# Putting neighbour lists into degree order on TensorE with one-hot matrices, and clearing an array later

## The chip, the cores and the metric

The kernel runs on one core of a Trainium2 chip. The core has five engines with instruction queues of their own: TensorE (PE), VectorE (DVE), ScalarE (ACT), GpSimd (POOL) and SyncE (SP); DMA transfers are issued by SP, ACT and POOL and carried out by 16 DMA engines. The metric is the device time of one execution in microseconds (us). The time before is the median of 14 runs.

## The reference

Two graph layers over 3327 nodes with 512 features each, on the same sparse 0/1 adjacency matrix (symmetric, with a diagonal of ones, some eight neighbours a node). Cut to what matters:

```python
# layer 0: attention over neighbours, 4 heads of 128
feats  = einsum('nf,hfo->hno', x, W)
logits = lrelu(e_s[:, :, None] + e_n[:, None, :], 0.2) + NEG_INF * (1 - A)
out    = softmax(logits) @ feats + b
x      = layernorm(x + relu(out))
# layer 1: a second attention and a plain neighbour sum, each with a gate
e    = where(adj != 0, exp(-lrelu(s_left[:, None] + s_right[None, :], 0.01)), 0)
x_a  = (e / (e.sum(1) + 1e-5)) @ (x @ W_sa)
x_b  = adj @ (x @ W_gcnb) + b_gcnb
x    = layernorm(x + sigmoid(attn_a * x_a + attn_b * x_b))
```

## The kernel before

The kernel turns the adjacency matrix into lists of neighbours and then gathers rows by these lists, instead of multiplying by the matrix.

**Phase 0** reads the adjacency matrix in 7 chunks of 512 columns (the last has 256), each in 13 loads on SP's queue into 12 buffers (`at`). For each chunk PE multiplies the ones by powers of two (`make_codes`), ACT copies the sums, PE turns them (`turn_codes`), and DVE takes the largest 24 entries, decodes them and writes the neighbours' numbers into `st` (`top_codes`, `decode`, `pick`, lines 355 to 412). `st` holds for each node (partition = node within a tile of 128, second index = tile) its own number (word 0), up to 24 neighbours (words 1 to 24), its place in the group (word 25) and four attention terms of its own (words 26 to 29). Between these steps PE makes the feature rows (`features`, 26 tiles), which ACT copies out and POOL writes to `table0` in HBM; the order is the program's order on each engine (the loop at line 498), nothing is rescheduled.

**The order of degrees.** The nodes stand in two groups of 12 and 14 tiles. When the degrees of a group are known (`deg`), `rank_a` makes one-hot rows of them, and `rank_b` counts with two matrix products, a running sum on DVE and a few element-wise steps, until each node has its rank within the group (`ranki`). So tiles of nodes with like degrees come together, and each tile j needs `CAPS[j]` gathers only.

**What the lists go through.** `sort` scatters each tile's 128 rows of `st` (32 words) with one indirect DMA on POOL (`scatter`, line 137) to their ranks in a list in HBM, and one load (line 459) brings the list back as `srt`. For group 0 the scatters stand in `tasks`, of which three are issued after every feature tile (`later(3)` in `more`); the load is on POOL's queue, and behind it stand 12 gathers of the nodes' own rows of x (`own_x`). Group 0 is sorted in chunk 3 (`NC0`). For group 1 the rank comes after the last chunk; its scatters stand on POOL behind the first three tiles' gathers (`AHEAD`), and its load on SP.

**Layer 0** (loop at line 689) works through the 26 tiles in `order0`. For each tile POOL issues one indirect gather per list position (line 546) into 7 buffers of 6 rows, three tiles ahead; DVE makes the weights (`weigh_a`, `weigh_b`, lines 599 to 617), DVE and ACT multiply the gathered rows by them in place, and PE sums them up by products with the identity. Then come the norm and the columns that layer 1 needs, and the row is scattered to `table1`. **Layer 1** (loop at line 842) does the like from `table1`.

**A check on the side.** `over` has a one for each list position that a tile does not read; `covered` (line 468) multiplies it by `valid`, where a real neighbour stands there, and sets a flag that would start the dense version. `over` lies in a pool that takes the memory of `p0`, the pool of phase 0, and it is cleared and filled right after that pool's release (lines 676 to 678), ahead of the first `weigh_a` on DVE.

Of the kernel before, what the change touches and what calls it, by code (L numbers as in the profile page):

```python
# [8 lines left out]
F32 = mybir.dt.float32  # L9
# [5 lines left out]
P = 128  # L15
# [10 lines left out]
CAPS = (22, 12, 11, 10, 9, 9, 8, 8, 7, 6, 6, 5) + (22, 13, 11, 10, 10, 9, 9, 8, 8, 7, 7, 6, 5, 4)  # L26
LW = 32
ND = 25
# [48 lines left out]
def sparse_pass(  # L77
# [54 lines left out]
    own1 = dram.tile([NG[1] * P, 2, ROW], F32, name="own1")  # L132
    lists = [dram.tile([n * P, LW], I32, name=f"lists{i}") for i, n in enumerate(NG)]

# [13 lines left out]

    srt = [const.tile([P, n, LW], I32, name=f"srt{i}") for i, n in enumerate(NG)]
    ident = const.tile([P, P], F32, name="ident")  # L150
# [102 lines left out]
    )  # L253
    all1 = p0.tile([P, ND * NM], F32, name="all1")
    nc.gpsimd.memset(all1, 1.0)
    st = p0.tile([P, NT, LW], I32, name="st")
    nc.gpsimd.memset(st, 0)
    nc.gpsimd.iota(st[:, :, 0], pattern=[[P, NT]], base=0, channel_multiplier=1)
    for g, n in enumerate(NG):
        nc.gpsimd.iota(st[:, T0[g] : T0[g] + n, S + 1], pattern=[[P, n]], base=0, channel_multiplier=1)  # L260

    for s in range(2):
        for hh in range(2):
# [8 lines left out]
            nc.vector.tensor_reduce(w0[:, :, s, 2 * FO + 2 * hh : 2 * FO + 2 * hh + 2], prod, AX.X, ALU.add)  # L272
    zrow = p0.tile([1, ROW], F32, name="zrow")
    nc.gpsimd.memset(zrow, 0.0)
    nc.gpsimd.memset(zrow[:, F : F + 1], BIG)
    nc.gpsimd.dma_start(table1[N:NP, :], zrow)
    nrow = p0.tile([1, ROW], F32, name="nrow")
    nc.gpsimd.memset(nrow, 0.0)
# [28 lines left out]
    def features(t):  # L307

        i = t * P // CH
        xc = xcs[i]  # L310
        o = t * P - chunks[i]
        pf = psf.tile([P, 2, 512], F32, tag="pf", name=f"pf{t}")
        for k, hh in ((k, hh) for hh in range(2) for k in range(KT)):
            nc.tensor.matmul(  # L314
                pf[:, hh, :HC], xc[:, k, o : o + P], w0[:, k, hh, :], start=(k == 0), stop=(k == KT - 1)
            )
# [3 lines left out]
        nc.scalar.copy(st[:, t, S + 2 : S + 2 + H].bitcast(F32), pf[:, 1, F // 2 : HC])  # L320
# [105 lines left out]
    def rank_b(g):  # L426
# [10 lines left out]
        cum = p0.tile([P, ND * NM], F32, tag="cum", name=f"cum{g}")[:, :w]  # L437
        nc.vector.tensor_tensor_scan(cum, all1[:, :w], tots, 0.0, ALU.mult, ALU.add)
        nc.vector.tensor_sub(cum, cum, tots)
# [3 lines left out]
        nc.vector.tensor_reduce(rk[:, :n], cum.rearrange("p (v t) -> p t v", v=ND), AX.X, ALU.add)  # L443
        ranki = p0.tile([P, NM], I32, tag="ranki", name=f"ranki{g}", bufs=2)
        nc.vector.tensor_copy(ranki[:, :n], rk[:, :n])
        return ranki

# [6 lines left out]

    def sort(g, ranki, queue):

        put = lambda t: scatter(f"lists{g}", lists[g][:, :], ranki[:, t : t + 1], st[:, T0[g] + t, :])
        tasks.extend(lambda t=t: put(t) for t in range(NG[g]))
        tasks.append(lambda: queue.dma_start(srt[g], lists[g].rearrange("(t p) w -> p t w", p=P)))
        if g == 0:  # L460
# [7 lines left out]
    def covered():  # L468

        for g, n in enumerate(NG):  # L470
            nc.vector.tensor_scalar(valid[:, T0[g] : T0[g] + n, :], srt[g][:, :, 1 : S + 1], N, None, ALU.is_lt)
        bad = m0.tile([P, 4], F32, name="bad")
        nc.vector.tensor_reduce(bad[:, 0:1], ovf, AX.XY, ALU.max)
        nc.vector.tensor_scalar(bad[:, 0:1], bad[:, 0:1], 0.0, None, ALU.is_gt)
        nc.vector.tensor_mul(over, over, valid)
        nc.vector.tensor_reduce(bad[:, 1:2], over, AX.XY, ALU.max)
# [21 lines left out]
    for i in range(len(chunks)):  # L498
        make_codes(i)
        more(1)  # L500
        if i == NC0:
            rankis[0] = rank_b(0)
            sort(0, rankis[0], nc.gpsimd)
        turn_codes(i)
# [9 lines left out]
    rank_a(1)  # L514
    rankis[1] = rank_b(1)

    psf.release()
# [81 lines left out]
    def weigh_a(j):  # L599
        c = CAPS[j] + 1  # L600
        g, i = place(j)
        w = ws[j] = m0.tile([P, S + 1, H], F32, tag="w", name=f"w{j}", bufs=3)
        es = srt[g][:, i : i + 1, S + 2 : S + 2 + H].bitcast(F32)
        for s0, n, buf, o in got[j]:
# [61 lines left out]
    for i in range(AHEAD):  # L666
        got[order0[i]] = gather(table0, order0[i])
    sort(1, rankis[1], nc.sync)
    later(len(tasks))
    psl.release()  # L670
# [3 lines left out]
    over = x1b.tile([P, NT, S], F32, name="over")  # L674
    valid = x1b.tile([P, NT, S], F32, name="valid")
    nc.vector.memset(over, 0.0)
    for j, c in enumerate(CAPS):
        nc.vector.memset(over[:, j, c:S], 1.0)

# [9 lines left out]
    for i in range(NT + 3):  # L689
# [647 lines left out]
```

## Time and profile before

| what | us |
|---|---|
| median of 14 runs (1128.64 to 1154.78) | 1137.49 |
| the profiled execution | 1130.09 |
| its span, first to last instruction | 1128.4 |
| DVE busy | 733.0 (65%) |
| PE busy | 843.7 (75%) |
| POOL busy | 660.8 (59%) |
| ACT busy | 274.7 (24%) |
| last chunk picked, degrees of group 1 complete | 234.6 |
| ranks of group 1 ready | 241.0 |
| first weights of layer 0 | 262.3 |
| granted clock of PE, mean | 0.859 |

Times in the trace are counted from the first instruction. A row of a timeline has the start, the duration, the engine, the line of the kernel, the operation with the tiles that it writes and reads, the shapes, and in brackets the engine's idle time before it with what seems to have ended it; "issue" means that no event was found. Ends of matrix products are modelled. A busy share is a mean over stages with different limits.

### The profile page before, as it was taken

To read this page: it belongs to the slowest core of one execution; us is meant where nothing else is said; L and a number is where in the kernel's file an instruction comes from. 1 tells how busy PE (TensorE), PEld (TensorE's weight loads), DVE (VectorE), ACT (ScalarE), POOL (GpSimd) and SP (SyncE) were. 2 spreads that over 40 slices of the span, in tenths; PEclk is the share of its full clock that TensorE was granted. 3 is DMA by queue.
4 is the path that set the end of the run, shared out by engine and by line. 5 is a ranking of instruction groups with operands and counts; after the bars stand their busy time and mean duration, and the time that the engine had idled before them with its cause. 6 is when DMAs were issued, how large, how long until landed. Compare 5 with 4: busy or idle time off the path is not lost.

```text
span 1128.4 us, 10026 instructions
## 1 busy us (share of the span) xinstructions
PE 843.7 (75%) x2564; PEld 440.3 (39%) x2564; DVE 733.0 (65%) x2128; ACT 274.7 (24%) x751; POOL 660.8 (59%) x673
## 2 busy tenths in 40 slices
PE   5798862025976877987587975579896996999895
PEld 4576740012433433443244442234342442444342
DVE  4587786136565362832665685459796997989894
ACT  0121110002424231341143331122222122222322
POOL 7310437734666656677567527735766777777702
PEclk9898975557988888888698886779898998999998
DMA  9998999925766658667566616744867776666601
GB/s 323 395 382 344 360 386 370 330 39 145 195 176 185 180 161 199 185 186 235 170 190 203 195 57 182 199 112 121 193 169 188 179 188 190 178 182 187 181 29 59
DMA packets 74194, 229.31 MB, mean 203 GB/s; under 512 B 13873, under 2 KB 18145, under 8 KB 73233
## 3 DMA queue, kind: packets, MB, share of 16 engines
q0 software_dynamic: 50240, 164.52, 51.6%
q1 hardware_dynamic: 22784, 61.97, 14.6%
q10 hardware_dynamic: 1104, 2.10, 0.5%
q8 instruction: 23, 0.38, 0.1%
q14 instruction: 43, 0.34, 0.1%
HBM read 207.46 MB, written 28.54 MB: 209 GB/s over the span
## 4 chain that ended last, share of the span: by engine, by line
PE 24%; issue 15%; DVE 14%; another core or an unknown queue 8%; POOL 8%; ACT 5%; DMA 3%; DVEq 0%; POOLq 0%; ACTq 0%
PE acc L634 12%; POOL g L546 7%; DVE sw L795 6%; PE acc L812 4%; PE po L831 3%; DMA g<-table,srt 3%; ACT g L629 2%; PE pcol L650 2%; DVE g L797 2%; PE acc L623 2%; POOL out L137 1%; DVE g L631 1%; ACT xt L647 1%; PE pt L822 1%
## 5 line engine op out<-in xcount | busy, mean ns | idle before, releaser
L546 POOL DMA_INDIRECT g<-table,srt x496 | 509.5, 1027 | 245.6 <-issue 159.2
L634 PE MATMUL acc<-g,ident 128*128 128x512 f32 x536 | 251.5, 627 | 21.5 <-DVE g L631 21.5
L795 DVE SCALAR_TENSOR_TENSOR sw<-g,e,sw 128x512 f32<-128x512 f32 x242 | 181.4, 749 | 15.5 <-ACT sw L784 5.0
L634 PEld LDWEIGHTS acc<-g,ident 128*128 128x128 f32 x536 | 109.9, 205 | 167.2 <-issue 130.8
L812 PE MATMUL acc<-g,ident 128*128 128x512 f32 x294 | 137.3, 604 | 13.3 <-DVE g L797 12.1
L631 DVE TENSOR_TENSOR g<-g,w 128x512 f32<-128x512 f32 x188 | 117.9, 695 | 1.2 <-DVE w L617 0.6
L831 PE MATMUL po<-wsa,sT 128*128 128x512 f32 x208 | 101.5, 634 | 18.2 <-issue 18.0
L314 PE MATMUL pf<-w,xc 128*128 128x260 f32 x416 | 104.1, 414 | 13.4 <-DVE w L272 13.4
L629 ACT ACTIVATE g<-g,w 128x128 f32<-128x128 f32 x320 | 96.3, 390 | 1.9 <-DVE w L617 1.9
L314 PEld LDWEIGHTS pf<-w,xc 128*128 128x128 f32 x416 | 85.0, 207 | 30.0 <-DVE w L272 14.2
L650 PE MATMUL pcol<-v,xt 128*128 128x8 f32 x208 | 36.4, 303 | 79.2 <-ACT xt L647 66.0
L831 PE MATMUL po<-wg,sT 128*128 128x512 f32 x208 | 93.5, 592 | 0.0
L812 PEld LDWEIGHTS acc<-g,ident 128*128 128x128 f32 x294 | 56.2, 193 | 88.1 <-issue 62.3
L831 PEld LDWEIGHTS po<-wsa,sT 128*128 128x128 f32 x208 | 42.1, 204 | 75.8 <-issue 73.3
L797 DVE TENSOR_TENSOR g<-g 128x512 f32<-128x512 f32 x95 | 65.7, 691 | 3.3
L650 PEld LDWEIGHTS pcol<-v,xt 128*128 128x128 f32 x208 | 34.0, 248 | 85.4 <-ACT xt L647 70.3
L321 POOL DMA_DIRECT2D table<-row x26 | 14.4, 555 | 81.7 <-ACT st L320 81.7
L831 PEld LDWEIGHTS po<-wg,sT 128*128 128x128 f32 x208 | 39.5, 190 | 49.7 <-issue 48.8
L137 POOL DMA_INDIRECT out<-za,srt x26 | 28.5, 1095 | 48.3 <-ACT za L872 41.6
L647 ACT COPY xt<-x1t 128x512 f32<-128x512 f32 x26 | 15.2, 584 | 161.5 <-remote 82.3
L610 ACT ACTIVATE w<-w 128x40 f32<-128x40 f32 (+10 forms) x26 | 6.1, 236 | 195.0 <-DVE w L609 145.7
L824 ACT COPY sT<-pt 128x512 f32<-128x512 f32 x52 | 29.0, 587 | 87.2 <-remote 49.8
(186 smaller groups left out, 909.3 us busy)
## 6 DMA issues: line engine op xcount, KB each, us to landing
at<-in_adjB SPq DMA_DIRECT2D x78, 512.0 KB
g<-table,srt POOLq DMA_INDIRECT x496
table<-row POOLq DMA_DIRECT2D x26, 260.0 KB
xc<-in_xB SPq DMA_DIRECT2D x6, 1024.0 KB
own<-in_xo SPq DMA_DIRECT2D x1, 3640.0 KB
own<-table SPq DMA_DIRECT2D x1, 3640.0 KB
at<-in_adjL SPq DMA_DIRECT2D x13, 256.0 KB
w<-in_W0B SPq DMA_DIRECT2D x1, 1040.0 KB
```

What stands on the lines that cost most here:

```text
L137: put = nc.gpsimd.indirect_dma_start(out=dst, out_offset=bass.IndirectOffsetOnAxis(ap=rows, axis=0), in_=src, in_offset=None, bounds_check ...
L314: nc.tensor.matmul(pf[:, hh, :HC], xc[:, k, o : o + P], w0[:, k, hh, :], start=(k == 0), stop=(k == KT - 1))
L546: nc.gpsimd.indirect_dma_start(out=buf[:, q - q0, :], out_offset=None, in_=table[:, :], in_offset=bass.IndirectOffsetOnAxis(ap=srt[g][:, i ...
L629: nc.scalar.activation(gv[:, h, :], gv[:, h, :], AF.Copy, scale=w[:, s, h : h + 1])
L631: nc.vector.tensor_tensor(gv, gv, w[:, s, :].rearrange("p (h o) -> p h o", o=1).to_broadcast([P, H, FO]), ALU.mult)
L634: nc.tensor.matmul(acc, ident, buf[:, o + s - s0, 0:F], start=False, stop=(s == CAPS[j]))
L650: nc.tensor.matmul(pcol, xt1[:, k, :], v1[:, k, :], start=(k == 0), stop=(k == KT - 1))
L795: nc.vector.scalar_tensor_tensor(sw, g[:, i, 0:F], e[:, s : s + 1], sw, ALU.mult, ALU.add)
L797: nc.vector.tensor_add(g[:, i, 0:F], g[:, i - 1, 0:F], g[:, i, 0:F])
L812: nc.tensor.matmul(plain[j], ident, row, start=(not sums_of_two and i == 0), stop=(sums_of_two and i == len(rows) - 1),)
L824: nc.scalar.copy(sT, pt)
L831: nc.tensor.matmul(proj[j], sT[:, k, :], wt[:, k, :], start=(half + k == 0), stop=(half + k == KT))
```

## The change

A list is put into order by a product with a one-hot matrix. For each tile t of a group, `row_is` has a one where a node's rank within its new tile equals the column; `spread` has the tile's 30 words of `st` in the stretch of columns that belongs to the node's new tile and zeros elsewhere. Their product, summed over the tiles t in one bank of PSUM, is the whole group's lists in order: 12 products of 360 columns and 14 of 420, in float32. Two copies on DVE bring them to `srt` (26 words, as integers) and `e_self` (the four terms). The rank is taken apart into tile (shift by 7) and row (the low 7 bits).

The lists in HBM, the 26 scatters and the two loads go. Group 0's sort stands in chunk 3 right behind `rank_b(0)`, and group 1's behind `rank_b(1)`, ahead of the release of phase 0's pools; `tasks` keeps the own-row gathers alone. `st` becomes float32 with 30 words, `all1` goes, two constants (`columns`, `tiles_`) are made by POOL at the start, and the two padding rows move to another pool. `valid` goes; `over` is cleared and filled in layer 0's loop at step 12, and `covered` multiplies in one step.

```diff
-LW = 32
+LW = 30
...
-    lists = [dram.tile([n * P, LW], I32, name=f"lists{i}") for i, n in enumerate(NG)]
...
-    srt = [const.tile([P, n, LW], I32, name=f"srt{i}") for i, n in enumerate(NG)]
+    srt = [const.tile([P, n, S + 2], I32, name=f"srt{i}") for i, n in enumerate(NG)]
+    e_self = [const.tile([P, n, H], F32, name=f"e_self{i}") for i, n in enumerate(NG)]
...
-    all1 = p0.tile([P, ND * NM], F32, name="all1")
-    nc.gpsimd.memset(all1, 1.0)
-    st = p0.tile([P, NT, LW], I32, name="st")
-    nc.gpsimd.memset(st, 0)
+    st = p0.tile([P, NT, LW], F32, name="st")
+    nc.gpsimd.memset(st, 0.0)
...
+    columns = p0.tile([P, P], F32, name="columns")
+    nc.gpsimd.iota(columns, pattern=[[1, P]], base=0, channel_multiplier=0, **count)
+    tiles_ = p0.tile([P, NM, LW], F32, name="tiles_")
+    nc.gpsimd.iota(tiles_, pattern=[[1, NM], [0, LW]], base=0, channel_multiplier=0, **count)
...
-    zrow = p0.tile([1, ROW], F32, name="zrow")
+    zrow = pj.tile([1, ROW], F32, name="zrow")
...
-        nc.vector.tensor_tensor_scan(cum, all1[:, :w], tots, 0.0, ALU.mult, ALU.add)
+        nc.vector.tensor_tensor_scan(cum, ones[:, 0:1].to_broadcast([P, w]), tots, 0.0, ALU.mult, ALU.add)
...
-        return ranki
+
+        ti = p0.tile([P, NM], I32, tag="ti", name=f"ti{g}")
+        nc.vector.tensor_scalar(ti[:, :n], ranki[:, :n], 7, None, ALU.logical_shift_right)
+        nc.vector.tensor_scalar(ranki[:, :n], ranki[:, :n], P - 1, None, ALU.bitwise_and)
+        to = p0.tile([P, 2, NM], F32, tag="to", name=f"to{g}")
+        nc.vector.tensor_copy(to[:, 0, :n], ti[:, :n])
+        nc.vector.tensor_copy(to[:, 1, :n], ranki[:, :n])
+        return to
...
-    def sort(g, ranki, queue):
-
-        put = lambda t: scatter(f"lists{g}", lists[g][:, :], ranki[:, t : t + 1], st[:, T0[g] + t, :])
-        tasks.extend(lambda t=t: put(t) for t in range(NG[g]))
-        tasks.append(lambda: queue.dma_start(srt[g], lists[g].rearrange("(t p) w -> p t w", p=P)))
+    def sort(g, to):
+
+        n = NG[g]
+        sorted_ = psl.tile([P, CH], F32, tag="pc0", name=f"sorted{g}")[:, : n * LW]
+        for t in range(n):
+            row_is = p0.tile([P, P], F32, tag="row_is", name=f"row_is{g}_{t}", bufs=2)
+            nc.vector.tensor_scalar(row_is, columns, to[:, 1, t : t + 1], None, ALU.is_equal)
+            spread = p0.tile([P, NM, LW], F32, tag="spread", name=f"spread{g}_{t}", bufs=2)
+            nc.vector.scalar_tensor_tensor(
+                spread[:, :n], tiles_[:, :n], to[:, 0, t : t + 1],
+                st[:, T0[g] + t : T0[g] + t + 1, :].to_broadcast([P, n, LW]), ALU.is_equal, ALU.mult,
+            )
+            nc.tensor.matmul(
+                sorted_, row_is, spread[:, :n].rearrange("p t w -> p (t w)"), start=(t == 0), stop=(t == n - 1)
+            )
+        by_tile = sorted_.rearrange("p (t w) -> p t w", t=n)
+        nc.vector.tensor_copy(srt[g], by_tile[:, :, : S + 2])
+        nc.vector.tensor_copy(e_self[g], by_tile[:, :, S + 2 :])
...
-            nc.vector.tensor_scalar(valid[:, T0[g] : T0[g] + n, :], srt[g][:, :, 1 : S + 1], N, None, ALU.is_lt)
+            past = over[:, T0[g] : T0[g] + n, :]
+            nc.vector.scalar_tensor_tensor(past, srt[g][:, :, 1 : S + 1], N, past, ALU.is_lt, ALU.mult)
...
-        nc.vector.tensor_mul(over, over, valid)
...
-            sort(0, rankis[0], nc.gpsimd)
+            sort(0, rankis[0])
...
     rankis[1] = rank_b(1)
+    sort(1, rankis[1])
...
-    sort(1, rankis[1], nc.sync)
-    later(len(tasks))
...
-    valid = x1b.tile([P, NT, S], F32, name="valid")
-    nc.vector.memset(over, 0.0)
-    for j, c in enumerate(CAPS):
-        nc.vector.memset(over[:, j, c:S], 1.0)
...
+        if i == NG[0]:
+            nc.vector.memset(over, 0.0)
+            for j, c in enumerate(CAPS):
+                nc.vector.memset(over[:, j, c:S], 1.0)
```

More of the change, by code (lines that the diff above doesn't have):

```diff
@@ L253, in sparse_pass @@
     )
-    all1 = p0.tile([P, ND * NM], F32, name="all1")
-    nc.gpsimd.memset(all1, 1.0)
-    st = p0.tile([P, NT, LW], I32, name="st")
-    nc.gpsimd.memset(st, 0)
-    nc.gpsimd.iota(st[:, :, 0], pattern=[[P, NT]], base=0, channel_multiplier=1)
-    for g, n in enumerate(NG):
-        nc.gpsimd.iota(st[:, T0[g] : T0[g] + n, S + 1], pattern=[[P, n]], base=0, channel_multiplier=1)
+    count = dict(allow_small_or_imprecise_dtypes=True)
+    st = p0.tile([P, NT, LW], F32, name="st")
+    nc.gpsimd.memset(st, 0.0)
+    nc.gpsimd.iota(st[:, :, 0], pattern=[[P, NT]], base=0, channel_multiplier=1, **count)
+    for g, n in enumerate(NG):
+        nc.gpsimd.iota(st[:, T0[g] : T0[g] + n, S + 1], pattern=[[P, n]], base=0, channel_multiplier=1, **count)
+    columns = p0.tile([P, P], F32, name="columns")
+    nc.gpsimd.iota(columns, pattern=[[1, P]], base=0, channel_multiplier=0, **count)
+    tiles_ = p0.tile([P, NM, LW], F32, name="tiles_")
+    nc.gpsimd.iota(tiles_, pattern=[[1, NM], [0, LW]], base=0, channel_multiplier=0, **count)
     for s in range(2):
@@ L276, in sparse_pass @@
     nc.gpsimd.dma_start(table1[N:NP, :], zrow)
-    nrow = p0.tile([1, ROW], F32, name="nrow")
+    nrow = pj.tile([1, ROW], F32, name="nrow")
     nc.gpsimd.memset(nrow, 0.0)
@@ L319, in features @@
         nc.scalar.copy(row[:, F:ROW].rearrange("p (h o) -> p h o", h=2), pf[:, :, F // 2 : HC])
-        nc.scalar.copy(st[:, t, S + 2 : S + 2 + H].bitcast(F32), pf[:, 1, F // 2 : HC])
+        nc.scalar.copy(st[:, t, S + 2 : S + 2 + H], pf[:, 1, F // 2 : HC])
         nc.gpsimd.dma_start(table0[t * P : (t + 1) * P, :], row)
@@ L443, in rank_b @@
         nc.vector.tensor_reduce(rk[:, :n], cum.rearrange("p (v t) -> p t v", v=ND), AX.X, ALU.add)
-        ranki = p0.tile([P, NM], I32, tag="ranki", name=f"ranki{g}", bufs=2)
+        ranki = p0.tile([P, NM], I32, tag="ranki", name=f"ranki{g}")
         nc.vector.tensor_copy(ranki[:, :n], rk[:, :n])
-        return ranki
+        ti = p0.tile([P, NM], I32, tag="ti", name=f"ti{g}")
[5 more added lines that the diff above has]
+        return to
     tasks = []
@@ L602, in weigh_a @@
         w = ws[j] = m0.tile([P, S + 1, H], F32, tag="w", name=f"w{j}", bufs=3)
-        es = srt[g][:, i : i + 1, S + 2 : S + 2 + H].bitcast(F32)
+        es = e_self[g][:, i : i + 1, :]
         for s0, n, buf, o in got[j]:
```

## The prediction

> **What bounds the kernel now.** I read, in this order, the shares of the span, who waited for the scatters, the timeline around their end, and a table by stage. The shares name no single bound (PE 75%, DVE 65%, POOL 59%), so what counts is the place of the change: between the last degrees and the first attention tile.
>
> Instructions that write the lists, with what waits for them:
>
> ```profile
> L137 POOL DMA_INDIRECT lists<-st,ranki x26: 967/971/1066, 126.7 to 257.9; - x26
>   DVE over L676: 20.0, 1
>   POOL x1a L464: 6.7, 1
>   POOL srt L459: 2.2, 1
> ```
>
> The last two cost POOL alone (the load of `srt0` and the own-row gathers behind it); the first holds DVE for 20.0 us. The timeline of DVE shows what stands behind it (start, duration, instruction):
>
> ```profile
> 240.81 0.17 DVE L445 CAST ranki<-rk 128x14 int32<-128x14 f32 x1
> 261.03 0.58 DVE L676 MEMSET over<- 128x624 f32 x1 [20.05 <-issue]
> 262.23 0.14 DVE L684 COPY v1sum<-pv1sum 128x8 f32<-128x8 f32 x1
> 262.29 0.17 DVE L605 TENSOR_TENSOR w<-g,srt 128x24 f32<-128x24 f32 x1
> ```
>
> The last rank is ready at 240.98. The clearing of `over` waits for the second group's 14 scatters (241.27 to 258, landed by 260), and the first weights of layer 0 (L605) are queued behind it, although their gathers were issued from 179.25 to 224.4. So 21.5 us (240.81 to 262.29) are the price of the old way there.
>
> By stage (start:end, length, busy us and count of PE, PEld, DVE, ACT, POOL, granted PE clock, DMA share, GB/s):
>
> ```profile
> 124.00:144.00 20.00, 17.77 (x102) 13.95 (x102) 18.32 (x80) 4.26 (x14) 14.13 (x16) 1.00 0.92 343
> 144.00:165.00 21.00, 13.32 (x70) 7.85 (x67) 19.13 (x84) 2.85 (x10) 7.74 (x9) 0.77 1.03 389
> 165.00:183.00 18.00, 8.43 (x40) 3.43 (x40) 15.03 (x63) 1.63 (x3) 10.29 (x11) 0.50 1.06 385
> 183.00:230.00 47.00, 0.00 (x0) 0.00 (x0) 11.70 (x53) 0.00 (x0) 31.53 (x33) 0.50 1.02 321
> 241.00:262.00 21.00, 2.29 (x4) 0.71 (x4) 0.90 (x17) 0.00 (x0) 13.63 (x14) 0.50 0.10 18
> ```
>
> From 124 to 183 DVE has hardly a gap: it is the bound, at 0.25 us an instruction (84 in 21 us). From 183 to 230 it issues 53 instructions in 47 us, 0.89 us each, while the DMA engines are full of gathers and of the copies into `own1`; at 230 the traffic ends, and so does this. I call it the slow stretch; no row names its cause.
>
> **The first sort (group 0).** It stands after rank_b(0), ahead of the turning and picking of chunk 3, on both DVE and PE. What it takes from POOL (12 scatters, a load and its 6.7 us wait) held only the own-row gathers. What it adds to DVE: four small casts and shifts of about 0.2 us (as L445, 0.174) = 0.8; twelve pairs of a 128x128 comparison (L238, 0.217) and a 128x360 product. The latter from these rows, 1.1 ns an element, is 0.54:
>
> ```profile
> L441 DVE TENSOR_TENSOR cum<-cum,oh 128x350 f32<-128x350 f32 x1 | 0.5, 525 | 0.0
> L441 DVE TENSOR_TENSOR cum<-cum,oh 128x300 f32<-128x300 f32 x1 | 0.5, 470 | 0.0
> L238 DVE TENSOR_SCALAR less<-ident 128x128 bf16<-128x128 f32 x1 | 0.2, 217 | 0.0
> ```
>
> 12 x 0.75 = 9.0; the last product's end 0.9; two copies from PSUM 0.7. Sum 11.4. On PE a 300-column product took 0.50 from start to start here (L432 at 119.36, L434 at 119.86), so 360 columns take 0.60 and DVE sets the pace. At the lower clock of the later rank (350 columns, 1.37 to 1.50) it would be 1.4 to 1.5 and the sort 18; I take 11.4, since the clock is 1.00 in 124 to 144.
>
> PE is blocked as long, and it was not idle:
>
> ```profile
> 121.15 14.22 PE L314 MATMUL pf<-w,xc 128*128 128x260 f32 x64
> 135.30 1.30 PE L341 MATMUL pc<-at,pow 128*32 128x512 bf16 x17
> 143.49 1.11 PE L361 MATMUL pv<-ident,v 128*128 128x128 f32 x8
> ```
>
> The turning of chunk 3 began at 120.37 and would begin at about 134.3, 13.9 later. So chunk 4 reaches DVE at 143.5 + 13.9 = 157.5 (before 144.6; DVE itself is free at 156), and ends at 178. Chunk 5 began at 166.6, 1.5 us after DVE was free, when the last adjacency block had come; now it begins at 178.2, 11.6 late. SP's next loads wait for the buffers that chunk 4 frees 14 us later; the twelve own-row gathers (128 rows of 2 KB each, 3.1 MB in all) move into that hole. On POOL they are queued, three at a time, between the row writes of features 19 to 22, where the scatters (0.97 each) stood; they wait for `srt0` at 135, and so do these features for PE, so no row write is late by them.
>
> **The slow stretch.** It began after 508 counted DVE instructions (281 up to 124, then 80, 84, 63), and 53 + 18 more led to the last rank_a at 234.6. If it goes by instructions, the 30 new ones ahead of it bring it 7.5 us earlier in the program: it begins at 183 - 7.5 + 11.6 = 187, with 101 left. If it goes by the traffic it begins at 183; the result differs by 2. Its end: 226 if it goes with the gathers, which lose the own-row gathers ahead of them and start at about 174.5, 4.7 earlier; 244 if the whole traffic is 14 late. Of these 14, 9 are refilled by the own-row gathers (3.1 MB at 343 GB/s), so I take 230 + 5 = 235. Until then 48 / 0.89 = 54 instructions pass, and the other 47 take 0.25 each: rank_a(1) comes at 247 and not at 234.6, **+12.2**. By the same rule it is +6 for the early end and +19 for the late one.
>
> **The second sort.** From the last rank (CAST 0.17): shifts 0.8; fourteen pairs with 420 columns (0.60 + 0.22, less some 0.05 of overlap) 10.8; a cold start of PE 2.6; last product 0.9; copies 0.8. Then `v1sum`, whose products ran at 239.5 to 241.4 and now have to wait for the PSUM space that the sort reads last: 8 products, 1.85, and 0.2 with its copy. Sum 18.1 against 21.5: **-3.4**. The cold start is read from the next place where PE starts:
>
> ```profile
> 262.00:265.00 3.00, 0.18 (x1) 0.19 (x2) 2.50 (x24) 1.03 (x4) 0.00 (x0) 0.50 1.03 229
> 265.00:268.00 3.00, 3.00 (x4) 1.32 (x5) 2.57 (x10) 1.87 (x7) 0.00 (x0) 0.50 1.04 393
> 268.00:271.00 3.00, 3.00 (x8) 1.30 (x7) 2.93 (x7) 2.45 (x8) 0.00 (x0) 0.98 0.29 109
> ```
>
> PE works from 264.8 and has the full clock from 268, so three products go at 1.64 (1.37 / 350 x 420) and not at 0.77. Bounds: no cold start, -6; half clock throughout, as in 235 to 244 where broken PE work of 6.4 us left it at 0.50: 14 x 1.64 = 23 against 13.4, +6.
>
> The Trainium skill, "TensorE: Matmul & The Clock Gate", Part 1, says that about 3.4 us of sustained work release the clock, however many products that is. By it the cold start is 2.6 if DVE feeds PE without a pause, and the dear end, +6, if PE's short waits for DVE count as pauses, which that sentence leaves open.
>
> **The rest.** `over` is cleared at step 12 of layer 0's loop: 27 instructions, 0.58 + 0.61 + 0.07 = 1.3 us, between other DVE work; DVE is busy 234 of 414 us there, so I take 0.3, bounds 0 and 1.3. On SP the load of `srt1` goes, which waited until 260; the two weight loads behind it (issued at 260.9 and 261.4) come at about the sort's end, early in layer 0 as now, needed only in layer 1: 0. The removed `over` times `valid` product (0.80) stands at 674, beside the wait for layer 1's gathers: 0. The two new POOL iotas (about 1.2 us by L245's 0.99 for 350) hide in its 6.33 us wait for `a_row`, the moved `zrow` and `nrow` cost nothing, since their writes end before the gathers start; if not, their 0.8 us each would show at 175.
>
> **Sum.** 12.2 - 3.4 + 0.3 = **+9**. From the start of layer 0 on I let everything shift by this. Against the profiled execution (1130.09, span 1128.4) that is 1139; it stood 7.4 under the median of the 14 runs, and on the median 1137.49 I forecast **1146.5**. A measurement of this kernel tells about 0.5% (5.7 us) from no change.
>
> **Rivals.** (1) Faster: the slow stretch does not come back, or is short, because DVE reaches it at another instruction and the traffic stands differently. For it: 35 of its 47 us are no work. Against it: gathers and `own1` copies still run together. Price: chunk 5 ends at 198.4, chunk 6 at 211, ranks at 217.5, sort and `v1sum` at 235.5, instead of 262.3: -27, and -20 if the next such stretch falls into the second sort and holds until the gathers land (230). It decides once DVE loses under 20 us in the stretch and not 35. (2) The first sort is hidden: the stretch ends at 230 with the same work done, only -3.4 stays; within 0.5%. For it: the early end is set by POOL. (3) PE stays at half clock in both sorts: 18 - 11.4 = +7 in the first, +9 in the second, on top of the +9: +25, slower. For it: 0.50 from 165 to 265; against it: 1.00 where the first sort stands.
>
> A second rule would favour (1): the Trainium skill, "Runtime: NRT & Kernel Launch", Instruction fetch mechanics, calls the fetching of instruction blocks mostly hidden. No row here tells whether the slow stretch is late instructions; if it is, this trace shows a case that is not hidden, with 35 us. By the rule it would go, and rival (1) with -27 be the forecast.
>
> **How the numbers follow.** My forecast 0.52, with its own range of 0 (early end, no cold start: 6 - 6) to +21 (late end, and half of the second sort's dearer clock: 19 - 3.4 + 0.3 + 5); rival (1) 0.25, (2) 0.13, (3) 0.10. Slower by over 0.5%: 0.7 of the forecast and (3), 0.46. Within: the other 0.3 of it and half of (2), 0.22. Faster: 0.32. The range reaches from the middle of (1), -23, to the forecast's own end, +21, and a little over for (3): 1114 to 1160.
>
> **What would show it.** First sort: picking of chunk 3 starts at 135 and chunk 4's codes on PE near 149. The slow stretch: DVE counts in 185 to 235, and the last rank near 253. Second sort: first weights some 18 us behind the last rank, near 270, with no 20 us wait. The prediction is wrong if the last rank comes before 241.

## The result, and the profile after

The kernel after takes 1152.65 us (median; 1138.56 to 1160.11), the kernel before beside it 1137.39. The ratio is 1.0132, with a 95% interval of 1.0089 to 1.0175: slower by 1.3%, some 15 us. The profiled execution took 1148.89 us (span 1147.1), against 1130.09 (span 1128.4), so the two profiled executions stand 18.8 apart. In these two the change is spread thus:

| point, us from the first instruction | before | after | difference so far |
|---|---|---|---|
| picking of chunk 3 begins (DVE) | 123.8 | 137.4 | +13.6 |
| picking of chunk 4 begins | 144.6 | 164.0 | +19.4 |
| picking of chunk 5 begins | 166.6 | 184.9 | +18.3 |
| last rank ready to be cast (L445, L448 after) | 240.81 | 255.00 | +14.2 |
| first weights of layer 0 (L605, L629 after) | 262.29 | 274.48 | +12.2 |
| issue of the last output scatter | 1121.49 | 1133.20 | +11.7 |
| end of the span | 1128.35 | 1147.10 | +18.8 |

Three places hold all of it: the first sort, the second sort, and the last microseconds of the program.

**The first sort.** The timeline of PE in the kernel after (start, duration, line, instruction; in brackets PE's idle time before it and its releaser):

```profile
125.32 11.54 PE L477 MATMUL sorted<-spread,row_is 128*128 128x360 f32 x24 [4.82 <-DVE spread L473]
136.70 0.95 PE L364 MATMUL pv<-ident,v 128*128 128x128 f32 x8
137.49 14.22 PE L317 MATMUL pf<-w,xc 128*128 128x260 f32 x64
151.63 1.30 PE L344 MATMUL pc<-at,pow 128*32 128x512 bf16 x17
...
157.77 0.40 PE L344 MATMUL pc<-at,pow 128*32 128x512 bf16 x2 [4.12 <-DMA at<-in_adjB]
...
163.40 0.95 PE L364 MATMUL pv<-ident,v 128*128 128x128 f32 x8
```

Twelve products in float32 (24 matrix instructions) stand ahead of the turning of chunk 3 (136.70; 120.37 before), of 64 feature products and of chunk 4's codes (151.63; 135.30 before). Those codes free the buffers of the adjacency loads, so the loads come later too: PE waits 4.12 us for the last of chunk 4 (2.23 before), and chunk 4 reaches DVE at 164. DVE, which had no gap there before, stands idle:

```profile
163.99 0.40 DVE L69 MAX8 ent<-pv 128x8 f32<-128x224 f32 x1 [5.78 <-PE pv L364]
```

**The second sort.** DVE's timeline of the kernel after, from the last rank to the first weights:

```profile
255.00 0.17 DVE L448 CAST ranki<-rk 128x14 int32<-128x14 f32 x1
...
258.54 0.29 DVE L471 TENSOR_SCALAR row_is<-columns,to 128x128 f32<-128x128 f32 x1 [1.10 <-PE sorted L477]
...
271.78 0.54 DVE L481 CAST srt<-sorted 128x364 int32<-128x364 f32 x1 [1.06 <-PE sorted L477]
...
273.77 0.17 DVE L702 COPY v1sum<-pv1sum 128x8 f32<-128x8 f32 x1 [1.33 <-PE pv1sum L701]
274.48 0.18 DVE L629 TENSOR_TENSOR w<-g,e_self 128x24 f32<-128x24 f32 x1 [0.55 <-issue]
```

The 20.05 us wait is gone, and 19.5 us of work with short waits for PE (255.00 to 274.48) stand where 21.5 us stood.

**The end.** The last 10 us of the two spans, by stage table (columns as in the prediction), before and then after:

```profile
1118.30:1128.30 10.00, 0.00 (x0) 0.00 (x0) 1.72 (x11) 0.81 (x1) 1.96 (x2) 0.50 0.21 84
```
```profile
1137.00:1147.00 10.00, 0.00 (x0) 0.00 (x0) 0.00 (x0) 0.00 (x0) 0.00 (x0) 0.50 0.00 0
```

In the kernel after, no engine computes and no DMA moves in these 10 us. The trace's record of POOL shows what passes then, although the page counts it as no busy time: behind the last output scatter (issued 1133.20) the closing semaphore step takes 2.00 us in place of 0.62, and the closing DRAIN 7.42 in place of 1.78. From the last scatter's issue to the end it is 13.9 us, and was 6.9. These 7.0 us belong to no operation of the kernel and to no term of the prediction.

### The profile page after: what moved, and what is told of

Its sections match the earlier page's. It is cut to its first block, busy times and chain, and to the rows that moved or that the text cites. A ratio compares the mean times of both kernels' runs of the same rounds, so it can differ in the third digit from the quotient of the medians.

```text
span 1147.1 us, 10200 instructions
## 1 busy us (share of the span) xinstructions
PE 866.6 (76%) x2616; PEld 447.8 (39%) x2616; DVE 755.7 (66%) x2191; ACT 275.8 (24%) x751; POOL 628.0 (55%) x647
## 3 DMA queue, kind: packets, MB, share of 16 engines
q1 hardware_dynamic: 20976, 61.74, 14.4%
## 4 chain that ended last, share of the span: by engine, by line
PE 29%; DVE 18%; issue 16%; another core or an unknown queue 13%; POOL 11%; DMA 7%; ACT 5%; POOLq 0%; DVEq 0%; ACTq 0%
PE acc L658 10%; POOL g L570 9%; PE pf L317 9%; DVE sw L817 6%; DMA at<-in_adjB 3%; PE po L853 2%; DMA g<-table,srt 2%; DVE g L819 2%; ACT g L653 2%; PE acc L834 2%; PE sorted L477 2%; PE acc L647 2%; PE pcol L674 1%; DMA a_row<-in_a_self 1%
## 5 line engine op out<-in xcount | busy, mean ns | idle before, releaser
L570 POOL DMA_INDIRECT g<-table,srt x496 | 503.1, 1014 | 293.9 <-issue 158.0
L853 PE MATMUL po<-wsa,sT 128*128 128x512 f32 x208 | 104.7, 651 | 14.6 <-issue 12.7
L324 POOL DMA_DIRECT2D table<-row x26 | 14.4, 552 | 107.6 <-ACT st L323 107.6
```

The costliest lines, as they stand in the source:

```text
L570: nc.gpsimd.indirect_dma_start(out=buf[:, q - q0, :], out_offset=None, in_=table[:, :], in_offset=bass.IndirectOffsetOnAxis(ap=srt[g][:, i ...
L853: nc.tensor.matmul(proj[j], sT[:, k, :], wt[:, k, :], start=(half + k == 0), stop=(half + k == KT))
```

## The experiments

The kernels ran in three groups, each on one chip with the kernel before beside it. The groups are not alike: the kernel before took 1032.3 us beside the first group, 1032.4 beside the second, and 1134.6 beside the third (1137 in the first measurement). So ratios are read within a group, and the profiles show what differs between them. The marks of all profiled executions, with which the verdicts below work (us; the tail is from the last output scatter's issue to the end of the span, DRAIN is the last long instruction of POOL's queue, and the ratio is to the kernel before beside it; the profiled execution of e9_before_pad2 was a long one, 1146.3 us where its median is 1133.1):

| kernel | last rank | first weights | last scatter | tail | DRAIN | ratio |
|---|---|---|---|---|---|---|
| before, first measurement | 240.8 | 262.3 | 1121.5 | 6.9 | 1.78 | |
| after, first measurement | 255.0 | 274.5 | 1133.2 | 13.9 | 7.42 | 1.0132 |
| group 1: e1_late | 204.8 | 206.2 | 1014.1 | 6.7 | 1.78 | 0.9909 |
| e2_early | 225.1 | 244.9 | 1021.2 | 14.0 | 7.42 | 1.0063 |
| e3_late_pe0 | 224.9 | 226.2 | 1022.2 | 15.1 | 8.56 | 1.0089 |
| e4_late_pe1 | 206.5 | 226.4 | 1001.9 | 16.2 | 9.30 | 0.9890 |
| group 2: c_before | 205.8 | 246.7 | 1022.1 | 6.7 | 1.78 | |
| c_after | 225.1 | 245.3 | 1022.1 | 13.8 | 7.42 | 1.0050 |
| e5_own_late | 223.2 | 242.5 | 1020.6 | 7.9 | 2.28 | 0.9985 |
| e7_spread | 205.0 | 206.4 | 1009.7 | 6.7 | 1.78 | 0.9885 |
| group 3: e8_after_pad3 | 257.0 | 277.0 | 1124.1 | 14.4 | 7.50 | 1.0190 |
| e9_before_pad2 | 241.3 | 262.2 | 1137.8 | 6.6 | 1.78 | 0.9992 |
| e10_pe1_pad6 | 243.2 | 262.7 | 1132.1 | 5.7 | 0.72 | 1.0017 |
| e11_sort0_later | 257.6 | 277.4 | 1138.6 | 13.9 | 7.42 | 1.0182 |

My theory at the outset: the change loses in the first sort, which stands in the queues of DVE and PE, wins little in the second, and its only cheap part is the late clearing. The rivals were that another wait takes the place of the one removed, that the second sort loses the time, and that the traffic sets the end of phase 0 anyway.

### Late clearing alone (e1_late)

```diff
-    nc.vector.memset(over, 0.0)
-    for j, c in enumerate(CAPS):
-        nc.vector.memset(over[:, j, c:S], 1.0)
...
+        if i == NG[0]:
+            nc.vector.memset(over, 0.0)
+            for j, c in enumerate(CAPS):
+                nc.vector.memset(over[:, j, c:S], 1.0)
```

> The kernel before, with one part of the change alone: over is cleared and filled at step 12 of layer 0's loop; both sorts stay scatters and loads. My theory: only the early clearing waits for group 1's 14 scatters (the 20.05 us gap of DVE at 241 to 261), the gathers of the first tiles have long been issued, so the first weights come near 242 to 245 in place of 262.3 and the time falls by 15 to 20 us, ratio 0.983 to 0.987, which beats both kernels. Rival A: another wait takes its place (POOL's gathers of the fourth tile on stand behind the scatters until 258; PSUM of v1sum), the first weights come early but DVE then idles for gathers: ratio 0.995 to 1.00. Rival B: the slow stretch of DVE ends only with the scatters: first weights near 255, ratio 0.994.

Measured: 0.9909 (0.9879 to 0.9940), 9.5 us less, between the theory's figure and rival A's. The first weights come 1.4 us behind the last rank, as the theory had it: of what stands ahead of them on DVE, only the early clearing waited for the scatters. (That they come at 206 and not at 242 to 245 is because this chip has no slow stretch, see c_before.) But the wait of rival A is there too. DVE's waits from 204 to 290 in e1_late (in total, times, longest):

```profile
DVE w L605 <- DMA g<-table,srt: 30.5, 6, 12.4
DVE w L605 <- DMA lists<-st,ranki: 6.9, 1, 6.9
```

The 14 scatters still stand on POOL ahead of the gathers of the fourth tile and on, and DVE, with its first weights at 206 and not at 247 (c_before below), then waits 37 us.

### The changed kernel with early clearing (e2_early)

The same lines put back where they stood, in the kernel after.

> The changed kernel with over cleared and filled early, right after phase 0's pools are released. My theory: with the lists sorted on TensorE the early clearing waits for nothing that its followers don't wait for too, and costs its own 1.3 us: first weights near 275.5 in place of 274.5, against the kernel after 0 to +1.5 us, so some 1.014 of the kernel before. Rival: the late clearing is a part of its own worth; then the first weights come 5 us or more later and the ratio is 1.018 or more.

Measured: 1.0063 (1.0040 to 1.0086); the unchanged kernel after had 1.0050 (1.0022 to 1.0078) in the second group. The first weights come at 244.9 and 245.3. So the theory holds for the difference, as far as two chips can be compared: once the lists are sorted on TensorE, clearing late is worth nothing that can be measured. The level was wrong (1.006, not 1.014), because this chip does not have the slow stretch (see c_before).

### Group 0 alone on TensorE (e3_late_pe0)

Late clearing as in e1_late; `sort_pe` is the new sort, with two more copies to float32.

```diff
-            sort(0, rankis[0], nc.gpsimd)
+            sort_pe(0, rankis[0])
```

> The kernel before with over cleared late, and group 0 alone sorted on TensorE (two more DVE copies of some 0.5 us, since the lists stay integers); group 1 keeps its scatters. My theory: the first sort costs 14 us in the queues of DVE and PE, the adjacency loads of chunk 5 come that much later, and the last rank comes at 255 in place of 241; the first weights follow at once, near 256 to 258: 14 us behind the version with late clearing alone, and some 4 to 6 us (0.995) under the kernel before. Rival: phase 0 is set by the traffic, the last rank comes at 241 to 245, and the time is that of late clearing alone within 4 us.

Measured: 1.0089 (1.0062 to 1.0116), 17 us above e1_late. The last rank comes 20.1 us later (theory 14, rival under 4), so the traffic alone does not set the end of phase 0 here. By the last output scatter the loss has shrunk to 8.1 us, as e1_late waited for gathers meanwhile; but the tail adds 8.4. The forecast ratio (0.995) was missed by both.

### Group 1 alone on TensorE (e4_late_pe1)

```diff
-    sort(1, rankis[1], nc.sync)
-    later(len(tasks))
+    sort_pe(1, rankis[1])
```

> The kernel before with over cleared late, and group 1 alone sorted on TensorE (two more DVE copies of some 0.5 us); group 0 keeps its scatters. My theory: phase 0 is as before, the last rank at 241, and the sort with its cold PE takes 19 to 20 us: first weights near 260.5, 18 us behind late clearing alone and 0 to 3 us (1.000 to 0.997) under the kernel before. Rival: the second sort is the part that loses the time of the change: first weights at 265 or later, ratio over 1.005.

Late clearing and `sort_pe` are those of e3_late_pe0. Measured: 0.9890 (0.9863 to 0.9917). The first weights come 20 us behind e1_late's, as expected, and yet the last output scatter is issued 12.2 us earlier. The 14 scatters are gone from POOL, and DVE's wait for gathers in 204 to 290 falls from 30.5 us to this:

```profile
DVE w L640 <- DMA g<-table,srt: 5.6, 2, 3.0
```

So the second sort is the part that gains, through POOL's queue and not through the wait that it removes; neither theory had this. Of the 12.2 the tail takes 9.4 back. The first sort's price is found a second time in e2_early less e4_late_pe1: 17.0 us in the medians, 19.3 by the last scatter.

### Before and after on one chip (c_before, c_after)

Both unchanged.

> The kernel before, unchanged, for a profile on the same chip as the runs beside it. In the four earlier experiments the stretch in which DVE loses 35 of 47 us did not appear, in any order of the work. If it goes with the chip, it is absent or present here for all kernels of this group alike; absent, the last rank comes near 205 and the first weights near 226; present, near 241 and 262. If it goes with the program, it is present here and in the changed kernel whatever the chip.

> The changed kernel, unchanged. From the four earlier experiments (late clearing alone 0.991; with group 1's sort on TensorE 0.989; group 0's sort on TensorE 17 us dearer wherever it was added): 1.006 without the slow stretch, as with the early clearing (1.0063), within 1.5 us; the last rank some 20 us behind before's. With the slow stretch 1.013 as in the first measurement. Rival: the late clearing has a worth of its own in the changed kernel: 1.003 or less.

The slow stretch does not go with the program, and is absent here (last rank 205.8, as expected; the first weights near 226 were not, see below). It is present or absent in all profiles of a group alike, and each group is one chip at one time; "chip" stands for both in this document, since no run tells them apart. c_after has the ratio and the distance of 19.3 us in the last rank that were expected. Its interval (1.0022 to 1.0078) reaches below the rival's 1.003; what speaks against the rival is that the first weights come at 245.3 here and at 244.9 with early clearing. The first sort takes 14.5 us (123.2 to 137.7), and DVE waits 5.5 us for chunk 4 behind it. The stage table for 183 to 200, in the first measurement's kernel before and then in c_before, the same program:

```profile
183.00:200.00 17.00, 0.00 (x0) 0.00 (x0) 6.37 (x28) 0.00 (x0) 13.01 (x14) 0.50 1.03 361
```
```profile
183.00:200.00 17.00, 0.00 (x0) 0.00 (x0) 15.45 (x73) 0.00 (x0) 12.97 (x14) 0.50 1.02 370
```

POOL issues the same 14 gathers, DMA moves 361 and 370 GB/s, and DVE does 28 instructions on the one chip and 73 on the other. What is more, without the stretch the wait that the change removes is the longer one. DVE in c_before:

```profile
205.83 0.17 DVE L445 CAST ranki<-rk 128x14 int32<-128x14 f32 x1
245.44 0.58 DVE L676 MEMSET over<- 128x624 f32 x1 [39.44 <-issue]
```

The scatters stand behind the first three tiles' gathers on POOL, which end at 225.4 whatever DVE does, and run to 243.3. In c_after the last rank comes 19.3 later, the sort takes 20.2, and the first weights come at 245.25 against 246.70: 1.5 us gained, the whole first sort hidden. The last output scatter is issued at 1022.06 against 1022.11. The 5 us by which the kernel after is slower here (1.0050) lie in the tail: 13.8 against 6.7.

### The copies into own1 issued later (e5_own_late)

```diff
-    nc.sync.dma_start(own1[:, 0, :], xo)
-    nc.sync.dma_start(own1[:, 1, :], table0[NG[0] * P : NP, :])
...
         got[order0[i]] = gather(table0, order0[i])
+    nc.gpsimd.dma_start(own1[:, 0, :], xo)
+    nc.gpsimd.dma_start(own1[:, 1, :], table0[NG[0] * P : NP, :])
```

> The changed kernel with the two copies into own1 taken from SP's queue ahead of the second rank and put on POOL's queue behind the gathers of the first three tiles. Theory S (the copies, HBM to HBM beside the gathers, make the slow stretch): if the profile of before beside it has the stretch, here it is gone or under 10 us long, the last rank comes 20 us or more earlier than in the changed kernel, and the ratio is 0.985 to 0.995. Rival (the stretch comes from the gathers alone, or from something outside the program): the last rank moves by under 5 us and the ratio is that of the changed kernel within 0.004. If no kernel of the group has the stretch, the two agree within 0.004 either way.

Measured: 0.9985 (0.9960 to 1.0009), on a chip without the stretch, so theory S was not tested. The forecast for that case, agreement with c_after within 0.004, failed: the last scatter comes 1.5 us earlier, and the tail is 7.9 and not 13.8, though nothing but the place of two copies differs.

### The scatters spread over layer 0 (e7_spread)

Late clearing, and in place of issuing all of group 1's scatters ahead of the loop:

```diff
-    later(len(tasks))
...
             got[j] = gather(table0, j)
+        later(2)
...
         if i == NG[0]:
+            p0.release()
```

> The kernel before with late clearing, and the 14 scatters of group 1 spread over layer 0's first seven steps, two behind each tile's gathers, their load in the eighth, and phase 0's pool released at step 12; no sort on TensorE. My theory: in the version with late clearing alone DVE idled for 7, 12 and 5 us because the gathers of the fourth to sixth tiles stood behind the 14 scatters; spread, they hide in POOL's idle time (77% busy in layer 0's first stage), and the time falls by some 10 us below late clearing alone and group 1's sort on TensorE: ratio 0.978 to 0.985. Rival: POOL bounds layer 0, the 14 scatters cost 17 us wherever they stand, and the ratio stays at 0.988 to 0.992.

Measured: 0.9885 (0.9840 to 0.9930), the rival's figure, with an interval that just reaches the theory's; against e1_late, 4.4 us less by the last scatter, though on another chip. Spreading moves DVE's waits more than it removes them (from 204 to 414 it waits 72.3 us for gathers, and in e1_late 76.5 and 6.9 for the scatters), which speaks for POOL as a bound of layer 0, as e4_late_pe1 does.

### What sets the tail (e8_after_pad3, e9_before_pad2, e10_pe1_pad6)

```diff
         nc.gpsimd.dma_start(table0[t * P : (t + 1) * P, :], row)
+        if t == 8:
+            for k in range(3):
+                nc.gpsimd.dma_start(pad[k : k + 1, :], zrow)
```

In e9_before_pad2 the count is 2, in the kernel before; in e10_pe1_pad6 it is 6, in e4_late_pe1.

> The changed kernel with three more small DMAs on POOL's queue (each writes one 2 KB row into an array that nobody reads, behind the ninth feature tile). In the kernel after, POOL's closing drain takes 7.42 us (before: 1.78), and the span ends 13.8 us behind the last output scatter's issue (before 6.7). Over the runs so far the drain falls with the number of POOL's DMAs modulo 8: 624 (0) 9.30, 625 (1) 8.56, 611 (3) 7.42, 613 (5) 2.28, 638 (6) 1.78. Theory: it is set by that remainder and not by the work; with 614 (6) the drain is 1.78, the tail 6.7, and the time falls by 7 us: ratio 0.997 to 0.999 where the changed kernel had 1.005. Rival: the drain is owed to something else in the changed program (its length, the missing scatters): the tail stays at 13.8 and the ratio at 1.004 to 1.006.

> The kernel before with two more small DMAs on POOL's queue, 640 in all (remainder 0). Theory: the closing drain grows from 1.78 to 9.3 us, the tail from 6.7 to 15 or 16, and the time by 8 to 9 us, ratio 1.008 to 1.009, though all the work is done as early as before. Rival (the number of DMAs plays no part): tail 6.7, ratio 0.999 to 1.001.

> The version with late clearing and group 1 alone sorted on TensorE (0.989, drain 9.30, tail 16.2), with six more small DMAs on POOL's queue, 630 in all (remainder 6). Theory: tail 6.7, 9 us less, ratio 0.980 and so the fastest kernel of the study. Rival: ratio stays at 0.989.

The remainder is refuted twice. With 614 DMAs the drain stays at 7.50 and the tail at 14.4 (1.0190, 1.0138 to 1.0241); with 640 it stays at 1.78 and the tail at 6.6 (0.9992, 0.9963 to 1.0021). Neither ratio of e8 came true: with the slow stretch on this chip, the two variants of the kernel after take 1.018 and 1.019 of the kernel before. Yet with six more small DMAs e10's drain is 0.72 and its tail 5.7, where e4_late_pe1, on another chip, had 9.30 and 16.2; and in e5_own_late, beside c_after, two copies more on POOL's queue took the drain from 7.42 to 2.28. So it moves with what POOL has issued in the program, by a rule that these runs don't give. Three things are shown: it does not go with the chip (7.42 in the kernel after on two chips and in two variants, 1.78 in the four programs that keep all 26 scatters); it is no wait for transfers, since in c_after the last data packet has landed 2.6 us before the drain begins; and it rises with the closing semaphore step ahead of it (0.36 to 0.72, 0.62 to 1.78, 2.00 to 7.42, 2.46 to 9.30). What the drain works off stays open.

e10_pe1_pad6 itself, 1.0017 (0.9976 to 1.0058), is not the fastest kernel: on this chip, with the slow stretch, its last rank and first weights (243.2, 262.7) are those of the kernel before, and the gain of e4_late_pe1 is gone: there the sort (20 us) took the place of a wait of 39 us (as in c_before), here of one of 20.

### The first sort one chunk later (e11_sort0_later)

```diff
         if i == NC0:
             rankis[0] = rank_b(0)
+        if i == NC0 + 1:
             sort(0, rankis[0])
```

> The changed kernel with the first sort moved one chunk on: the ranks of group 0 are worked out in chunk 3 as now, but the sort stands in the pass of chunk 4, behind that chunk's codes, so PE turns chunk 3 and makes chunk 4's codes ahead of it. My theory of the first sort's price where DVE has no slow stretch (last rank 225.1 against 205.8): 13.8 us are the sort's own time on DVE, and 5.5 are DVE's wait for chunk 4 at 164, which comes because PE, and with it the adjacency loads, were held behind the sort. With the move the second part goes: last rank near 219.5, first weights near 240, the time 5 us under the changed kernel (0.999 to 1.001; the closing drain stays at 7.42, since POOL's DMAs are as many). Rival: the loads come late all the same, since chunk 5's codes now stand behind the sort: last rank at 224 to 226, ratio 1.004 to 1.006.

Measured: 1.0182 (1.0125 to 1.0238), on a chip with the stretch. The step that the theory named is there: DVE begins chunk 5 at 177.0, where the kernel after began at 184.9, a gain of 7.9 (5.5 expected), and the 5.8 us gap at 164 is gone. But the slow stretch begins earlier by more, and takes it all back. Stage tables of the kernel after and of e11_sort0_later:

```profile
183.00:200.00 17.00, 6.97 (x39) 2.97 (x37) 13.72 (x55) 1.16 (x2) 11.56 (x12) 0.50 1.06 369
200.00:236.00 36.00, 0.80 (x3) 0.45 (x3) 5.92 (x32) 0.47 (x1) 22.84 (x24) 0.50 1.02 325
```
```profile
183.00:200.00 17.00, 1.60 (x6) 0.73 (x5) 5.38 (x22) 0.47 (x1) 12.73 (x15) 0.50 1.03 372
200.00:236.00 36.00, 0.00 (x0) 0.00 (x0) 5.22 (x28) 0.00 (x0) 22.59 (x24) 0.50 1.03 315
```

DVE does 55 instructions in 183 to 200 in the one and 22 in the other; from 200 to 236 both crawl (32 and 28). The last ranks come at 255.0 and 257.6 (257.0 in e8_after_pad3, on the chip of e11). On such a chip, then, what DVE saves ahead of the stretch is worth nothing if the stretch begins earlier with it. The theory's price on a chip without the stretch was not measured.

## Why the prediction was right, point by point

The forecast was +9 (12.2 - 3.4 + 0.3); measured are +15 (+10 to +20 by the interval), and in the profiled executions +18.8: 14.2 at the last rank, -2.0 in the second sort, -0.5 in layers 0 and 1, +7.0 in the tail. The sign of each of the first two steps was right, the loss was taken 2.0 too small and the gain 1.4 too large; the tail was missing; and the whole holds for a chip with the slow stretch only. That the time lies within the range (-23 to +22) says little, since the range holds "faster" and "slower" alike.

- **First sort, 11.4 us.** It took 13.8 (123.64 to 137.41). The pair of `row_is` and `spread` was sized at 0.75 and took 0.89 (seven pairs from 128.95 to 135.15): the comparison 0.29 where a row with bf16 output had given 0.22, the 360-column product 0.59 where 0.54 had been worked out; from start to start the two take 0.82, and the rest is waiting (see the second sort). And PE was at half clock, which I had excluded because the table gave 1.00 for 124 to 144. In the kernel after (granted clock is the third number from the end):

```profile
125.00:127.00 2.00, 1.68 (x3) 1.16 (x4) 1.04 (x4) 0.00 (x0) 0.00 (x0) 0.50 1.03 419
127.00:129.00 2.00, 1.94 (x5) 0.55 (x4) 1.55 (x5) 0.00 (x0) 0.00 (x0) 0.66 1.03 412
129.00:131.00 2.00, 1.94 (x5) 0.84 (x6) 1.82 (x6) 0.00 (x0) 0.00 (x0) 1.00 1.02 408
```

  DVE waited 0.96 and 0.41 us for these products. The table was that of the kernel before, where PE has no pause at this place. The change makes one: PE waits 4.82 us (120.50 to 125.32) for DVE to finish the rank and the first `spread`, and when it starts again the clock is 0.50.
- **PE blocked 13.9, chunk 4 on DVE at 157.5, chunk 5 at 178.2.** Measured: the turning of chunk 3 is 16.3 later, chunk 4 comes at 164.0 and chunk 5 at 184.9. This is the term most wrong in size: 18.3 late in place of 11.6. I had the own-row gathers fill the hole in the traffic; they did so only in part, since DMA moved 235 GB/s in 138 to 165 where the kernel before had 384, and the adjacency loads, held by their buffers, came late.
- **Slow stretch from 183 or 187 to 235, rank_a(1) at 247.** Measured: 199 to 236, and 248.8. The end was right, which is what counted; but that was luck. I had given its shift of 5 to the traffic and had the gathers of the first three tiles start 4.7 earlier, since no row write would be late. With PE blocked the last feature row is written to `table0` at 172.42 and not at 162.88, and the first gather is issued at 184.99 and not at 179.25; in all six profiles with the stretch it ends 6.8 to 8.1 behind the issue of the last of these gathers (229.12; before 223.42). Besides, chunk 5 came 6.7 later than I had it and the stretch began 12 to 16 later, which offset each other. Of the start neither rule was right: it goes neither by DVE's instructions nor by the time since the start.
- **+12.2 at the last rank.** Measured +14.2.
- **Second sort, 18.1 against 21.5.** Measured 19.5 against 21.5, so -2.0 and not -3.4. The mis-sized term is the pair: 0.96 and not 0.77 even with PE at full clock (six pairs from 263.26 to 269.02). DVE's own time for it, from start to start, is 0.85, and before every second pair DVE waits 0.22 for PE. `row_is` and `spread` have two buffers each: a pair can start when the product two before it is done, 1.01 after that product's start (262.25 to 263.26), and its own product starts 0.91 later (264.17); that is 1.92 for two pairs. In the first sort the same sum is 0.91 + 0.84 = 1.75 (128.97, 129.88, 130.72). I had asked which of the two engines sets the pace, and it is the way round through both. Whether a third buffer would bring the pair to DVE's own time was not tried. The start at half clock cost DVE 2.2 us of waits (1.10, 0.55, 0.55) where I had 2.6. That agreement is luck: half clock from 264.8 to 268 in the rows shown is two products of 1.64, not three.
- **Clearing in the loop +0.3, the rest 0.** By the last scatter the loss is 11.7 after 12.2 at the first weights, so layers 0 and 1 added nothing that shows. How little this pair of executions says of 0.3 us is seen from e8_after_pad3, where the way from the first weights to the last scatter takes 847.0 us and not the 858.7 of the kernel after, for the same work but three small DMAs. But the tail added 7.0: "from the start of layer 0 on I let everything shift" is the step that failed.
- **Rivals.** (2), the first sort hidden, was given 0.13; its outcome is what happens on the chip of the second group, by a path that I had not seen (POOL's gathers hold the scatters, so the old wait grows as much as the ranks come earlier). (1), the stretch gone, came true there as to the stretch, but for both kernels, and so gave no -27. (3), half the clock throughout, did not happen: it is 0.50 for 3 to 6 us of each sort. That the stretch is late instructions, which the prediction left open, is not what the trace's records of DMA packets suggest: in the kernel before no packet fetches instructions between 164.8 and 231.2, while DVE goes on executing, and the packet at 231.2 comes after about as many DVE instructions as the one at 197.7 in c_before (563 and 571). And from the rule cited there it would not follow that the stretch goes: a stretch with another cause stays.

The Trainium skill, "TensorE: Matmul & The Clock Gate", Part 1, speaks of about 3.4 us of sustained work ahead of the full clock, counted in time and not in products. One sort comes near it, the others take longer: the matrix instructions reach their short duration (0.47 and 0.52 us for the quicker ones, from 0.81 and 0.91) 3.1 and 4.9 us after the first one in the kernel after, 5.6 and 5.8 in c_after, and until then they follow one another without a pause. The dear end of the prediction, half clock throughout because of PE's waits for DVE, is refuted: the waits of some 0.1 us between later products left the clock at full.

## What to carry to other kernels

Before moving work off a queue that only waits, ask what is queued behind it on the engines that take it over: here the first sort had held nothing back on POOL and made the last rank 14 to 20 us later on DVE and PE, while the part that paid (group 1's scatters, where there is no slow stretch) paid through POOL's queue for gathers and not through the wait that the profile named. A wait that is removed is worth its length only if the next thing is there: without the slow stretch, late clearing removed a wait of 39.4 us (c_before) and gave 9.5. And compare the last microseconds of two spans too, where no line of the program stands: the whole loss on one chip was there.

## What was not expected of the hardware

- The same program on two chips: 28 DVE instructions in 17 us on one and 73 on the other, at the same traffic. In the stretch DVE's waits end on a grid of 0.70 us (in the kernel before at 183.71, 185.11, 185.83, 187.23, 187.94). In the six profiles that have it, it begins within 3.1 us of where SP has issued the second copy into `own1`, in two of them ahead of it (183.1, 200.8, 201.9, 182.2, 182.2 and 187.4; first gaps of DVE over 0.9 us, other than for PE, at 185.1, 199.4, 202.5, 183.9, 185.3 and 186.2), and ends between 230 and 237, 6.8 to 8.1 us behind the issue of the last gather of the first three tiles. The same copies and gathers on two other chips don't bring it. Whether moving the copies ends it was tried only where it doesn't occur, so its cause stays open.
- The stretch is not all that differs between the chips. From the first weights to the last output scatter the kernel before takes 859.2 us on the first chip and 775.4 in c_before, more than the 35 us at the last rank. At the same step of layer 0, a copy on DVE behind a product that starts at 302.76 and at 287.00 and takes 1.06 (first chip, then c_before):

```profile
313.46 0.17 DVE L654 COPY x1a<-pcol 128x8 f32<-128x8 f32 x1 [10.14 <-issue]
```
```profile
288.09 0.17 DVE L654 COPY x1a<-pcol 128x8 f32<-128x8 f32 x1 [0.53 <-PE pcol L650]
```

  After 262 us, idle times over 3 us that no recorded event ends come 10 times on DVE, 24 on ACT and 6 on PE in the one (93, 189 and 31 us in all), and in c_before once on DVE (4.7 us). The six profiles with the stretch have 31 to 40 of them each, the other eight at most one. So where the stretch occurs, engines start late in layers 0 and 1 too, and what is special to phase 0 can't be the whole cause.
- POOL's closing drain takes 0.72 to 9.30 us by what POOL issued earlier, and is counted in the time.
- No version beats both kernels on every chip that was seen. Group 1 alone on TensorE (0.9890) and the spread scatters (0.9885) do where the stretch is absent; with it, the former, its tail shortened, is even with the kernel before; the latter was not run there. Late clearing alone was not run on such a chip.
